# A four-layer graph network on one core: a planner's constants, the first transfers, and the last graph by halves

## The chip, the cores and the metric

The kernel runs on one core of a Trainium2 chip. The metric is the device time of one execution in microseconds, as the median of several runs. The engines are TensorE (PE, with its weight loads as PEld), VectorE (DVE), ScalarE (ACT), GpSimd (POOL) and SyncE (SP), which issues the transfers.

## The reference, cut to what matters

There are 32 independent graphs of 512 nodes with 256 features, each with an adjacency of 512 x 512, all in float32. Every graph goes through four layers, each with a residual and a layer norm:

```python
agg = einsum('bnm,bmd->bnd', adj, x)
# layer 0
x = layernorm(x + relu(((1 + eps) * x + agg) @ W1 + b1) @ W2 + b2)
# layer 1
h = adj @ (x @ W.T + b);  x = layernorm(x + where(h > 0, h, alpha * h))
# layer 2
h = layernorm(x) * g + be
x = layernorm(x + x + relu((adj @ h) @ W_rel + b_rel + h @ W_root))
# layer 3
h = ((epsilon * x + agg) @ W1 + b1)
h = silu(h * rsqrt(mean(h * h) + 1e-6) * w)
x = layernorm(x + h @ W2 + b2)
```

## The kernel before

**Recorded operations and a planner.** The kernel does not issue its instructions as it goes. Every helper (`mm`, `act`, `add`, `mul`, `ts`, `stt`, `copy`, `inv_sqrt`) records an `Op` in a `Plan`, with the engines that could do it and a cost for each; every transfer is recorded by `move`. At the end `Plan.order` goes through time, always takes the engine that is free first, and gives it the recorded operation of the lowest rank among those that can start. `copy` and the scaling of a norm may go to DVE or ACT, all else has one engine. The kernel then issues all operations in the order found, so all of them carry one source line (L295 for operations, L313 for transfers). On the chip each engine keeps that order and waits at semaphores.

**Rank.** An operation's rank is its graph's number times a `period`, plus the time by which `needs` wants it, reckoned back from the matmuls that wait for it. After the graph called `final`, the graphs are spaced by `last` instead of `period`. `RULES` holds pairs of such settings (period, pace, last, near); `best` plans with each and keeps the one whose last operation starts earliest. Up to five graphs (`FLIGHT`) are in work at once, so one graph's matmuls cover another's elementwise work. In `needs` an operation inherits a due time only from consumers of its own graph; graph -1 holds what comes ahead of the first graph, in the kernel before nothing but nine matmuls on zeros.

**Powers and the port.** A norm's inverse square root is a power on POOL (`inv_sqrt`, a tensor_tensor with -0.5). The planner holds back DVE operations with two operands outside PSUM (`TWO_OPERANDS`) for `PORT` microseconds after a DVE operation that feeds a power, so that the power starts undisturbed, and while a power's input is being taken the power holds off in turn. Where DVE has nothing else to do in that time, the planner notes a `pause`, and the kernel issues small memsets to the tile `pause` in its place (L1168).

**Matrix products.** All products go through `seven`, a scheme of seven products of half-size blocks in place of eight. `right_sums` and `left_sums` make the needed sums of blocks on DVE, `take` and `put` bring results out of PSUM. `aggregate` multiplies by the adjacency, `dense_feat` and `dense_add` are the dense layers. `with_loops` adds the self loops (`loop0` = identity times 1 + eps, `loop3`) to the diagonal blocks of the adjacency.

**The start.** SP first issues the adjacency of graph 0 in four transfers of 256 KB, then x in one of 512 KB, then the epsilon of layer 0 (0.5 KB), then weights. DVE makes `one_eps0` and `loop0` from epsilon.

**The end.** In the first and the last graph (`alone()`) layer 3 takes its row norm by `everywhere` with a power and four transposing matmuls on `ident` ("flips"), and its last norm with `NormOnVector` (batch-norm statistics on DVE). `dense_add` calls `norm.half(h)` as each half of the tokens is done, half 1 first; then `norm.scales` makes one power for all four chunks, `norm.scaled` scales them, and one transfer of 512 KB writes the graph.

Of the kernel before, what the change touches and what calls it, by code (L numbers as in the profile page):

```python
# [11 lines left out]
AF = mybir.ActivationFunctionType  # L12
ALU = mybir.AluOpType
# [3 lines left out]
LN_EPS = 1e-5  # L17
# [3 lines left out]
def span(ap):  # L21

    n = 1
    for d in ap.shape[1:]:
        n *= d
    return n
# [13 lines left out]
def vector_time(n):  # L40
    return 0.06 + n * 0.00106, 0.085
# [20 lines left out]
def power_time(n):  # L62
    return 0.3 + n * 0.18, 0.2 + 0.06 * n
# [13 lines left out]


TWO_OPERANDS = ("tensor_add", "tensor_sub", "tensor_mul", "scalar_tensor_tensor")
PORT = 0.35  # L80


SOON = 0.03
# [3 lines left out]

RULES = [(42, 2, 20, 0.5), (42, 2, 12, 0.25)]


class Pool:
# [122 lines left out]
class Plan:  # L218
# [102 lines left out]
    def needs(self, pace, near):  # L321

        work, need = {}, []
        for op in self.ops:
            t = op.ways.get("tensor")
            need.append(work.get(op.graph, 0.0) * pace if t else 1e3)
            if t:
                work[op.graph] = work.get(op.graph, 0.0) + t[0][0]  # L330
        between = [20.0] * len(self.ops)
        for i in range(len(self.ops) - 1, -1, -1):
            op = self.ops[i]
            cost = min(sum(w[0]) for w in op.ways.values()) + 0.1
            for n, _ in op.then:
                if self.ops[n].graph == op.graph:
                    need[i] = min(need[i], need[n] - cost)
                    step = 0.0 if "tensor" in self.ops[n].ways else between[n] + cost
                    between[i] = min(between[i], step)
        return [  # L340
            t if "tensor" in op.ways else t + near * b
            for op, t, b in zip(self.ops, need, between)
        ]

    def best(self):


        rule = min(RULES, key=lambda rule: self.order(*rule)[0])
        return self.order(*rule)[1]

    def order(self, period, pace, last, near):

        final = max(op.graph for op in self.ops) - self.flight + 1
        rank = [
            (min(op.graph, final) * period + max(op.graph - final, 0) * last + need, i)
            for i, (op, need) in enumerate(zip(self.ops, self.needs(pace, near)))
# [14 lines left out]
        done = []  # L371
        while can_start:
# [31 lines left out]
            for i in can_start:  # L404
                op = self.ops[i]
# [17 lines left out]
            op = self.ops[i]  # L423
# [4 lines left out]
            if engine == "vector":  # L428
# [4 lines left out]
                if any(n in powers for n, _ in op.then):  # L433
                    port["vector"] = t + busy + PORT
            if op.kbytes:
# [23 lines left out]
def tile_gnn_stack(ctx: ExitStack, tc: tile.TileContext, a: dict, out: bass.AP):  # L459
# [26 lines left out]
    B, N, D = a["x"].shape  # L486
    NC = N // P
# [5 lines left out]
    HC = NC // 2  # L493
# [8 lines left out]
    plan = Plan(nc, FLIGHT)  # L502
# [24 lines left out]
    def vector(method, n, *args, **kw):  # L527
        return "vector", method, vector_time(n), args, kw

    def scalar(func, n, x, times=scalar_time, **kw):  # L530
        columns = sum(k in ("scale", "bias") and not isinstance(v, float) for k, v in kw.items())
        return "scalar", "activation", times(n, columns), (x,), dict(func=func, **kw)

    def mm(o, lhsT, rhs, first, last):
        kw = dict(start=first, stop=last, skip_group_check=True)
        way = "tensor", "matmul", matmul_time(rhs.shape[-1]), (lhsT, rhs), kw
        plan.do(o, way, ordered=o.room)
# [13 lines left out]
    def add(o, x, y):  # L551
        plan.do(o, vector("tensor_add", span(o), x, y))
# [4 lines left out]
    def mul(o, x, y):  # L557
        plan.do(o, vector("tensor_mul", span(o), x, y))

    def ts(o, x, s1, s2, op0, op1=None):  # L560
        kw = dict(op0=op0) if op1 is None else dict(op0=op0, op1=op1)
        plan.do(o, vector("tensor_scalar", span(o), x, s1, s2, **kw))
# [9 lines left out]
    def inv_sqrt(o, x):  # L572
        n, p = span(o), o.shape[0]
        plan.do(
            o, ("gpsimd", "tensor_tensor", power_time(n), (x, mhalf[0:p, 0:n]), dict(op=ALU.pow))
        )
# [11 lines left out]
    def bank(*shape):  # L588
        return Part(Room(banks)).shaped(*shape)

    def tok():
        return room(NC, D)

    def half(t, h):
        return t[:, h * HC : (h + 1) * HC]
# [16 lines left out]
    def constant(name, shape):  # L612
        return const.tile(shape, F32, tag=name, name=name)
# [15 lines left out]
    def weight(name):  # L629
        w = a[name]  # L630
        t = constant(name, [P, w.shape[0] // P, w.shape[1]])
        size = w.shape[0] * w.shape[1] / 256
        plan.move(t, w.rearrange("(c p) f -> p c f", p=P), size)
        return t
# [5 lines left out]
    scraps = [constant(f"scrap{i}", [P, D]) for i in range(2)]  # L640
# [206 lines left out]
    def dense_add(x, right, left, done):  # L847


        def block(i, j):  # L850
            return x[:, j * HC : (j + 1) * HC, i * P : (i + 1) * P]

        def product(m, ps, first):
            n = len(right[m])
            for k in range(n):
                for i in range(HC):
                    mm(
                        ps[:, i, :], right[m][k][:, i * P : (i + 1) * P], left[m][:, k, :],
                        first and i == 0 and k == 0, k == n - 1,
                    )  # L860

        def take(ps, i, j):
            add(block(i, j), ps, block(i, j))

        def put(ps, i, j, more):
            take(ps, i, j)
            if i == 1:
                done(j)

        seven(*(bank(HC, P) for _ in range(3)), product, take, put)  # L870
# [22 lines left out]
    class Norm:  # L893
# [24 lines left out]
        def scales(self, *affine):  # L918
# [5 lines left out]
            n = len(affine) * NC  # L924
            inv_sqrt(self.rstd[:, 0:n], self.ve[:, 0:n])

        def scaled(self, i=0):

            y = self.r if i == self.last else tok()
            s, shift = (t[:, i * NC : (i + 1) * NC] for t in (self.rstd, self.shift))  # L930
            mul(shift, self.less, s)
            for c in range(NC):
                r, scale = self.r[:, c, :], s[:, c : c + 1]
                plan.do(
                    y[:, c, :],
                    vector(
                        "tensor_scalar", D, r, self.less[:, c : c + 1], scale,
                        op0=ALU.add, op1=ALU.mult,
                    ),
                    scalar(AF.Identity, D, r, scale=scale, bias=shift[:, c : c + 1]),  # L940
                )
            return y

    class NormOnVector(Norm):
# [58 lines left out]
    def plus_row(x, r):  # L1003

        for h in range(2):
            add(half(x, h), half(x, h), r.unsqueeze(1).to_broadcast([P, HC, D]))
# [12 lines left out]

    def load_x(b):  # L1020
        x = tok()
        plan.move(x, a["x"][b].rearrange("(p c) d -> p c d", c=NC), N * D / 256, late=1.6)
        return x

    def layer0(x, adjacency):
# [53 lines left out]
    def layer3(x, adjacency, b):  # L1079

        aT = aggregate(x, adjacency)
        plus_row(x, b2_3)
        hT, acc = Wide(FC3), short(N)

        def squares(f):
            sq = room(2, N)
            act(sq, hT.pair(f), AF.Square)
            if f == 0:
                add(acc, sq[:, 0, :], sq[:, 1, :])
            else:  # L1090
                add(acc, acc, sq[:, 0, :])
                add(acc, acc, sq[:, 1, :])

        dense_feat(aT, A1_3, b1_3, hT, squares)
        pr = everywhere(column_sums(acc), (1.0 / HID3, RMS_EPS, ALU.mult, ALU.add))
        right = {}
        for q in range(0, FH, 2):
            for f in (q, q + 1, FH + q, FH + q + 1):
                mul(hT.chunk(f), hT.chunk(f), pr)
                act(hT.chunk(f), hT.chunk(f), AF.Silu, scale=w_3[:, f : f + 1])  # L1100
            for m, t in dense_sums([hT.pair(q)], [hT.pair(FH + q)]).items():
                right[m] = right.get(m, []) + t
        norm = (NormOnVector if alone() else Norm)(x)
        dense_add(x, right, A2_3, norm.half)
        norm.scales((1.0, LN_EPS))
        y = norm.scaled()
        place = out[b].rearrange("(p c) d -> p c d", c=NC)
        plan.move(place, y, N * D / 256, into=f"out{b}")

# [1 line left out]
    idle, zeros = bank(D), scraps[0]  # L1113
    for _ in range(9):
        mm(idle, zeros[:, 0:P], zeros, True, True)
    plan.graph = 0
    scraps = cycle(scraps)
    eps0 = row("L0_gnn_eps")
    x = load_x(0)
    adjacency = Adjacency(0)  # L1120
    one_eps0 = constant("one_eps0", [P, 1])
    ts(one_eps0, eps0, 1.0, None, ALU.add)
    loop0 = constant("loop0", [P, P])
    ts(loop0, ident, one_eps0, None, ALU.mult)
    W1_0 = weight("L0_gnn_W1")
    A1_0 = weight_sums("A1_0", *quarters(W1_0))
    b1_0 = col("L0_gnn_b1")
# [8 lines left out]
    x = layer0(x, adjacency)  # L1136
# [9 lines left out]
    h = layer1(x, adjacency)  # L1146
# [9 lines left out]
    A2_3 = weight_sums("A2_3", *blocks_of(W2_3[:, 0:FH], W2_3[:, FH:]))  # L1156
    layer3(layer2(*h, adjacency), adjacency, 0)
    for b in range(1, B):
        plan.graph = b
        x, adjacency = load_x(b), Adjacency(b)  # L1160
        h = layer1(layer0(x, adjacency), adjacency)
# [45 lines left out]
```

## Time and profile before

| | us |
|---|---|
| median of 3 runs | 2337.26 |
| lowest and highest | 2336.43, 2342.0 |
| the profiled execution, device time | 2338.08 |
| its span, from first to last instruction | 2336.3 |

The profiled execution is 0.8 us above the median. The page names the busy time of each engine and the costliest groups; since nearly all operations share a line, groups are told apart by the tiles that they write and read: `ps` is a PSUM bank, `room` a large tile of the work pool, `few` a small one for a norm's columns, `scrap` the unused output of an ACT sum. One matmul instruction makes two records in the trace. An idle time in square brackets is the engine's gap ahead of the instruction, with what ended it.

### The profile page before, as it was taken

The page shows a single profiled execution, that of the slowest core. Times are in us where ns is not written, and L with a number is a line of the kernel's source. Part 1 is how long each engine was busy: PE and PEld are TensorE (multiplying, and loading weights), DVE is VectorE, ACT ScalarE, POOL GpSimd, SP SyncE. Part 2 cuts the span into 40 slices and gives each one's busy share as a digit, 9 for nine tenths or more (in the row PEclk, how much of TensorE's full clock was granted, in tenths as well). Part 3 has the DMA queues.
Part 4 walks back from the last instruction along what each step waited for, and adds up shares of the span by engine and source line. Part 5 has one row for each costly group of instructions (what it writes and reads, how often), then busy time and mean ns, then how long its engine had stood idle before and what let it go on. Part 6 is the DMA issues. An engine that isn't in the chain of part 4 may idle for free.

```text
span 2336.3 us, 41057 instructions
## 1 busy us (share of the span) xinstructions
PE 2304.8 (99%) x14002; PEld 2105.4 (90%) x14002; DVE 2139.5 (92%) x5411; ACT 1630.1 (70%) x4409; POOL 261.9 (11%) x166
## 2 busy tenths in 40 slices
PE   9899999999999999999999999999999999999997
PEld 7798999999999999999999999999999999898997
DVE  8998999999999999999999999999999999899987
ACT  4676677766776776777767767767777677676775
POOL 0001101101101101011011011010110101101110
PEclk9999999999999999999999999999999999999999
DMA  7002122122221122211222211222112222121001
GB/s 239 19 19 57 24 57 54 28 56 62 57 60 28 56 57 64 55 47 37 57 62 57 60 27 56 57 63 56 44 38 58 62 60 58 23 65 55 15 17 39
DMA packets 223458, 122.83 MB, mean 53 GB/s; under 512 B 142864, under 2 KB 194320, under 8 KB 223248
## 3 DMA queue, kind: packets, MB, share of 16 engines
q1 hardware_dynamic: 223248, 120.20, 18.8%
q8 instruction: 111, 1.82, 0.3%
q14 instruction: 99, 0.81, 0.1%
HBM read 78.92 MB, written 24.97 MB: 44 GB/s over the span
## 4 chain that ended last, share of the span: by engine, by line
PE 73%; DVE 22%; issue 2%; ACT 2%; DMA 1%; POOL 0%; SPq 0%; DVEq 0%; POOLq 0%; ACTq 0%
PE ps L295 73%; DVE room L295 19%; DVE few L295 2%; ACT room L295 1%; ACT scrap L295 1%; DMA L_gnn_W<-in_L_gnn_W_dram 0%; DMA L_gnn_ln_beta_c<-in_L_gnn_ln_beta_dram 0%; POOL few L295 0%; DMA room<-in_adj_dram 0%; SPq L313 0%; DVE A L295 0%; DVEq L295 0%; POOLq L1203 0%; DVE L_gnn_W_root L295 0%; DVE pause L1168 0%
## 5 line engine op out<-in xcount | busy, mean ns | idle before, releaser
L295 PE MATMUL ps<-room,room 128*128 128x256 f32 x3584 | 920.1, 382 | 6.1 <-DVE room L295 1.9
L295 DVE TENSOR_TENSOR room<-room,room 128x512 f32<-128x512 f32 (+1 forms) x1360 | 783.4, 594 | 7.2 <-ACT room L295 4.4
L295 DVE TENSOR_TENSOR room<-ps,room 128x256 f32<-128x256 f32 (+1 forms) x1344 | 611.1, 470 | 143.3 <-PE ps L295 134.3
L295 PEld LDWEIGHTS ps<-room,room 128*128 128x128 f32 x3584 | 625.6, 191 | 73.7 <-DVE room L295 10.0
L295 PE MATMUL ps<-L_gnn_W,room 128*128 128x128 f32 (+1 forms) x3584 | 539.5, 291 | 6.5 <-ACT room L295 4.5
L295 PEld LDWEIGHTS ps<-L_gnn_W,room 128*128 128x128 f32 x3584 | 505.1, 192 | 39.2 <-ACT room L295 5.7
L295 POOL TENSOR_TENSOR few<-few,mhalf 128x4 f32<-128x4 f32 (+2 forms) x160 | 261.1, 1638 | 2068.7 <-DVE few L295 1969.4
L295 PEld LDWEIGHTS ps<-A,room 128*128 128x128 f32 x3072 | 453.5, 191 | 37.3 <-DVE room L295 3.7
L295 PE MATMUL ps<-A,room 128*128 128x128 f32 x3072 | 467.3, 275 | 1.6 <-DVE room L295 1.5
L295 PE MATMUL ps<-room,L_gnn_W 128*128 128x256 f32 x1536 | 419.8, 381 | 0.6 <-DVE room L295 0.5
L295 ACT ACTIVATE room<-room,few 128x256 f32<-128x256 f32 x590 | 316.7, 595 | 114.2 <-DVE few L295 113.1
L295 ACT ACTIVATE room<-room 128x1024 f32<-128x1024 f32 (+2 forms) x260 | 241.5, 941 | 165.2 <-DVE room L295 159.5
L295 ACT ACTIVATE room<-ps,L_gnn_b_c 128x256 f32<-128x256 f32 x768 | 309.9, 476 | 49.2 <-PE ps L295 42.2
L295 ACT ACTIVATE room<-ps 128x256 f32<-128x256 f32 (+1 forms) x515 | 180.6, 377 | 232.5 <-PE ps L295 231.5
L295 PE MATMUL ps<-room,A 128*128 128x256 f32 x1152 | 332.6, 381 | 5.5 <-ACT room L295 5.4
L295 DVE TENSOR_TENSOR room<-room 128x256 f32<-128x256 f32 (+1 forms) x640 | 312.9, 498 | 10.6 <-ACT room L295 3.0
L295 PEld LDWEIGHTS ps<-room,L_gnn_W 128*128 128x128 f32 x1536 | 276.3, 191 | 34.9 <-DVE room L295 2.5
L295 ACT ACTIVATE scrap<-room 128x256 f32<-128x256 f32 x504 | 206.7, 411 | 93.9 <-DVE room L295 84.2
L295 ACT ACTIVATE scrap<-room,few 128x256 f32<-128x256 f32 x504 | 251.9, 502 | 27.4 <-DVE few L295 25.4
L295 PEld LDWEIGHTS ps<-room,A 128*128 128x128 f32 x1152 | 198.9, 191 | 23.3 <-ACT room L295 6.7
L295 ACT ACTIVATE room<-room,L_gnn_rms_weight_c 128x512 f32<-128x512 f32 x256 | 173.6, 714 | 14.5 <-DVE room L295 14.3
L295 DVE TENSOR_TENSOR room<-room,loop 128x256 f32<-128x256 f32 x256 | 103.4, 411 | 4.1 <-PE ps L295 2.3
(57 smaller groups left out, 1131.7 us busy)
## 6 DMA issues: line engine op xcount, KB each, us to landing
room<-in_adj_dram SPq DMA_DIRECT2D x128, 256.0 KB, 5.1
room<-in_x_dram SPq DMA_DIRECT2D x32, 512.0 KB, 5.9
out_dram<-room SPq DMA_DIRECT2D x32, 512.0 KB, 3.1
room<-room SPq DMA_DIRECT2D x480, 32.0 KB, 2.0
diagonal<-room SPq DMA_DIRECT2D x62, 128.0 KB, 1.8
room<-in_adj_dram SPq DMA_DIRECT2D x124, 64.0 KB, 1.9
room<-diagonal SPq DMA_DIRECT2D x62, 128.0 KB, 2.2
room<-line SPq DMA_DIRECT2D x30, 256.0 KB, 3.2
```

The lines of the kernel that those rows point to most:

```text
L295: getattr(getattr(self.nc, engine), method)(to, *(put(x) for x in args), **kw)
```

## The change

Five edits in one:

1. `PORT` goes from 0.35 to 0.55.
2. The two `RULES` have `last` 10 and 16 in place of 20 and 12, both with `near` 0.5, and `final` is the highest graph less `LATE` = 3, so that graphs 29, 30 and 31 are spaced by `last` (before, four graphs).
3. The epsilon transfer, `one_eps0` and `loop0` are recorded in graph -1, and `needs` lets graph -1 inherit due times from any graph.
4. The first graph's x comes in two transfers of 256 KB.
5. The last graph finishes by halves: `finish` makes the scale, the power, the scaled chunks (`put`) and the transfer of each half as soon as its sums are there.

```diff
-PORT = 0.35
+PORT = 0.55
...
-RULES = [(42, 2, 20, 0.5), (42, 2, 12, 0.25)]
+LATE = 3
+RULES = [(42, 2, 10, 0.5), (42, 2, 16, 0.5)]
...
-                if self.ops[n].graph == op.graph:
+                if op.graph in (self.ops[n].graph, -1):
...
-        final = max(op.graph for op in self.ops) - self.flight + 1
+        final = max(op.graph for op in self.ops) - LATE
...
+        def finish(self, h, m, plus, place):
+
+            mine = slice(h * HC, (h + 1) * HC)
+            ve, rstd, shift = self.ve[:, mine], self.rstd[:, mine], self.shift[:, mine]
+            ts(ve, self.squares[:, mine], m / self.n, plus, ALU.mult, ALU.add)
+            inv_sqrt(rstd, ve)
+            mul(shift, self.less[:, mine], rstd)
+            for c in range(h * HC, (h + 1) * HC):
+                self.put(c, self.r, rstd[:, c % HC : c % HC + 1], shift[:, c % HC : c % HC + 1])
+            plan.move(place, half(self.r, h), N * D / 512, into=f"out{plan.graph}{h}")
...
-        plan.move(x, a["x"][b].rearrange("(p c) d -> p c d", c=NC), N * D / 256, late=1.6)
+        src = a["x"][b].rearrange("(p c) d -> p c d", c=NC)
+        if b:
+            plan.move(x, src, N * D / 256, late=1.6)
+        else:
+            for h in range(2):
+                plan.move(half(x, h), half(src, h), N * D / 512, late=1.6)
...
-        dense_add(x, right, A2_3, norm.half)
-        norm.scales((1.0, LN_EPS))
-        y = norm.scaled()
         place = out[b].rearrange("(p c) d -> p c d", c=NC)
-        plan.move(place, y, N * D / 256, into=f"out{b}")
+        if b < B - 1:
+            dense_add(x, right, A2_3, norm.half)
+            norm.scales((1.0, LN_EPS))
+            y = norm.scaled()
+            plan.move(place, y, N * D / 256, into=f"out{b}")
+        else:
+
+            def done(h):
+                norm.half(h)
+                norm.finish(h, 1.0, LN_EPS, half(place, h))
+
+            dense_add(x, right, A2_3, done)
...
-    plan.graph = 0
-    scraps = cycle(scraps)
     eps0 = row("L0_gnn_eps")
-    x = load_x(0)
-    adjacency = Adjacency(0)
     one_eps0 = constant("one_eps0", [P, 1])
     ts(one_eps0, eps0, 1.0, None, ALU.add)
     loop0 = constant("loop0", [P, P])
     ts(loop0, ident, one_eps0, None, ALU.mult)
+    plan.graph = 0
+    scraps = cycle(scraps)
+    x = load_x(0)
+    adjacency = Adjacency(0)
```

More of the change, by code (lines that the diff above doesn't have):

```diff
@@ L925, in scales, with put @@
             inv_sqrt(self.rstd[:, 0:n], self.ve[:, 0:n])
+        def finish(self, h, m, plus, place):
[7 more added lines that the diff above has]
+            plan.move(place, half(self.r, h), N * D / 512, into=f"out{plan.graph}{h}")
+        def put(self, c, y, scale, shift):
+            r = self.r[:, c, :]
+            plan.do(
+                y[:, c, :],
+                vector(
+                    "tensor_scalar", D, r, self.less[:, c : c + 1], scale, op0=ALU.add, op1=ALU.mult
+                ),
+                scalar(AF.Identity, D, r, scale=scale, bias=shift),
+            )
         def scaled(self, i=0):
@@ L932, in scaled @@
             for c in range(NC):
[L933 to L941, printed above, removed]
+                self.put(c, y, s[:, c : c + 1], shift[:, c : c + 1])
             return y
```

## The prediction

> **What bounds the kernel now.** I read the page first, then two steady windows, then the timeline where TensorE (PE) was idle.
>
> ```profile
> PE 2304.8 (99%) x14002; PEld 2105.4 (90%) x14002; DVE 2139.5 (92%) x5411; ACT 1630.1 (70%) x4409; POOL 261.9 (11%) x166
> ```
>
> ```profile
> 1210.91:1282.38 71.47, 71.39 (x436) 65.49 (x436) 66.01 (x167) 51.08 (x140) 8.46 (x6) 1.00 0.19 53
> 1282.38:1353.85 71.47, 71.39 (x436) 65.49 (x436) 66.03 (x167) 51.09 (x140) 8.46 (x6) 1.00 0.20 53
> ```
>
> The first line is the page's busy times. The columns of the two windows are length, then busy time of PE, its weight loads, DVE, ACT and POOL, then clock. One graph takes 71.47 us and PE is busy for 71.39 of it. In the trace a PE record of 256 columns follows the last after 216 ns, one of 128 columns after 112 ns; the program has 6810 and 7192 of them, so 1471 + 806 = 2277 us of pure streaming. The span is 2336.3, so **about 59 us are stalls**. One steady graph has 212 and 224 records, 45.8 + 25.1 = 70.9 us, so it loses only 0.6, some 15 us over 25 graphs. The rest lies at the two ends. What can be won is there; what can be lost is mostly in the middle, because anything lost per graph is multiplied.
>
> The losses at the start, from the timeline (start, length, engine, operation, idle before it and its releaser):
>
> ```profile
> 9.22 0.15 DVE L295 TENSOR_SCALAR one_eps<-L_gnn_eps 128x1 f32<-128x1 f32 x1 [3.60 <-DMA L_gnn_eps<-in_L_gnn_eps_dram]
> ...
> 11.38 3.72 PE L295 MATMUL ps<-room,room 128*128 128x256 f32 x16 [1.64 <-DVE room L295]
> ```
>
> DVE stands still for 3.60 us because a half-kilobyte vector lies behind 1.5 MB in the queue, and PE gets its second operand only at 11.38. Later, around 100 us:
>
> ```profile
> 100.93 0.46 ACT L295 ACTIVATE room<-ps,L_gnn_b_c 128x256 f32<-128x256 f32 x1
> ...
> 104.62 0.46 ACT L295 ACTIVATE room<-ps,L_gnn_b_c 128x256 f32<-128x256 f32 x1
> ...
> 105.13 2.08 PE L295 MATMUL ps<-room,A 128*128 128x256 f32 x4 [5.11 <-ACT room L295]
> ```
>
> and a window behind it, clock third from the end:
>
> ```profile
> 104.90:108.30 3.40, 3.17 (x8) 2.54 (x9) 3.01 (x11) 3.40 (x11) 1.36 (x1) 0.50 0.00 0
> ```
>
> PE waits 5.11 us for the second of two evictions of a bank by ACT; six norm sums stand between the two on ACT. Then the clock is granted at 0.50 for 3.4 us (the window), which costs another 1.7. At the end:
>
> ```profile
> 2306.29 2.05 PE L295 MATMUL ps<-L_gnn_W,room 128*128 128x128 f32 x16 [0.52 <-DVE room L295]
> ...
> 2310.13 0.65 PE L295 MATMUL ps<-ident,few 128*128 128x128 f32 x4 [1.79 <-POOL few L295]
> ...
> 2313.01 7.25 PE L295 MATMUL ps<-L_gnn_W,room 128*128 128x128 f32 x48 [2.23 <-ACT room L295]
> ...
> 2326.14 2.05 PE L295 MATMUL ps<-L_gnn_W,room 128*128 128x128 f32 x16 [0.52 <-DVE room L295]
> ...
> 2331.38 1.09 ACT L295 ACTIVATE room<-room,few 128x256 f32<-128x256 f32 x2 [5.38 <-DVE few L295]
> 2332.50 0.33 SPq L313 DMA_DIRECT2D out_dram<-room  x1
> ```
>
> In the last graph PE waits for the row norm's power, for the SiLUs behind it, and for DVE. After the four flips of `everywhere` only that graph's 56 output products are left, so nothing fills the waits.
>
> **What the Trainium skill says.** "TensorE: Matmul & The Clock Gate" (What's actually happening) says that an idle window of some 3.4 us halves the clock until PE has been busy for about as long. The trace agrees: 0.50 in 104.9 to 108.3 after the 5.11 us wait. "SBUF — State Buffer" (Who interferes with whom) says that a DVE instruction with two SBUF inputs contends with a GpSimd one that reads SBUF. The trace agrees, rarely: a power of four columns takes 1.01 us as a rule, but 2.32 at 283.54 and 2.04 at 2035.94, both beside DVE adds of two SBUF tiles. This is what PORT plans around.
>
> **The change part by part.** The order of both programs on every engine shows what the planner makes of it.
>
> *Epsilon first, x in halves.* The epsilon transfer is now SP's first issue, `one_eps0` and `loop0` are DVE's first work. Epsilon goes ahead of the adjacency by one issue, 0.43 us, and x is one issue more, 0.43. Before, the second half of the adjacency was there by about 7.3 (ACT's third copy starts at 7.28); now about 7.7. Then four DVE operations lead to PE's second product: two of 512 columns and two of 256, 0.60 and 0.34 from start to start, 1.9 us: 9.6 instead of 11.38. I take **-1.7**. Bounds: 0, since the DMA engines are 84 to 87% busy through the first 50 us and later loads may set the pace, and -2.2. DVE is 98% busy from 25 to 100 us, which is why I believe that an earlier DVE survives.
>
> *The order around 100 us.* PE's instructions up to the wait are the same products in the same order. On ACT the first of the two evictions moves ahead of its norm sums, and the second moves ahead of six sums that stood before it. In the old times the second would start when the sums now left ahead of it are over, at about 101.3 instead of 104.62. **-3.4** (bounds 0, if PE then waits for DVE, which was 92% busy there, and -5.1, if the half clock goes too).
>
> *The last three graphs at 10, from graph 29 on.* The planner chose period 20 before and chooses 10 now. Behind the flips 93 products of 128 columns now follow instead of 56: 37 of other graphs, 37 x 0.223 = 8.3 us of filler, 10 of them (2.2 us) before the first one that needs a SiLU. Ahead of the flips stand some 50 products of the other two graphs. So the waits of 0.68, 1.95 and 2.39 us (by start to start) and the 1.7 of half clock at 2313 go, 6.7 in sum; about 1.0 comes back, since two multiplications of 0.60 and two SiLUs of 0.65 on a queue take 3 us against 2.2 of filler. The last 0.68 stays. **-5.7**. Bounds -6.7 and -2: 24 norm sums (0.46 from start to start), 14 scalings (0.5) and 8 SiLUs (0.65) of three graphs now stand on ACT at once, about 23 us beside 21 of PE.
>
> *Norm and output by halves.* From the last product to the end were 8.1 us. The last power has two columns instead of four (1.01 us for four, 1.64 for eight, so about 0.7, -0.3) and ACT scales one chunk instead of two behind it (-0.5). But the neighbouring graph's three chunks now stand ahead of it on ACT (+0.9), its 512 KB ahead of the last 256 KB (+0.3), and two small DVE operations are added (+0.15). **+0.5**, bounds -1 and +1. Out by halves alone would save; its cover is gone because the other graphs end in the same 5 us.
>
> *PORT 0.55.* It is a number in the planner. 22 memsets of `pause` become 72: one per graph through the middle, 33 in DVE's last 600 of 4979 rows. Each takes 0.10 to 0.18 us of DVE. In the middle DVE has 5.5 us free per graph and is relieved of one operation that goes to ACT: 0. In the last stretch 33 x 0.15 = 5 us of DVE, where graphs bunch: before, the bunching at 2032 to 2040 already cost PE 1.1 + 1.5 and a half-clock window. I take **+1.5**, bounds -3 (some powers are no longer held up) and +8.
>
> *The middle.* The planner's order no longer repeats with every graph but with every second one; PE's order agrees with the old one for about 88%. DVE is level with PE in 14 us of each graph (the chain runs over DVE from 1268 to 1282, over PE for 55). Taken as **0**; it cannot gain over 0.6 x 25 = 15.
>
> Sum: -1.7 - 3.4 - 5.7 + 0.5 + 1.5 = -8.8 on the profiled execution's 2338.1, so 2329.3. The median of the runs is 0.8 below that execution: 2328.5, say **2329**.
>
> **Rivals.**
> 1. *Only the ends give.* The wait at 100 us returns under another name (bank, DVE) and the bunching eats half of the tail: -1.7 - 3.5 + 1 = -4, 2333. For it: DVE and ACT are both over 90% busy at 100 us. Against: ACT's order there is plainly better.
> 2. *The middle loses: slower.* The alternating order with a pause per graph adds waits to the 14 us where DVE and PE are level. It decides the sign where it exceeds 0.35 us per graph (8.8 / 25), and passes 0.3% from 0.63 us per graph, a doubling of today's loss. At 0.75 it gives 2328.5 + 19 = 2347. For it: the multiplier. Against: one DVE operation less, and evictions now go first behind the powers' producers.
> 3. *More than I count.* The half clock at 105 goes too and the middle sheds a third of its stalls: -8.8 - 1.7 - 5, 2322.
> 4. *The edits do little*: the first loads are bound by DMA, the tail by ACT: 2337. The order shows that the edits are made, so this is the far end of rival 1.
>
> **How the numbers follow.** 0.3% of 2337 is 7.0 us, about what a measurement of this kernel can tell from no change: faster means below 2330.2, slower above 2344.3. Forecast 0.50 (2323 to 2334; four fifths of it faster); rivals 1 and 4 together 0.28 (2331 to 2340, nearly all the same); rival 3 0.10; rival 2 0.12. Faster 0.40 + 0.03 + 0.10 = 0.53, same 0.10 + 0.25 = 0.35, slower 0.12. The range 2321 to 2341 leaves out most of rival 2 and the edge of rival 3.
>
> **What would show it.** One_eps before 4 us, PE's second product before 10; no PE wait over 2.5 us at 100; a steady pair of graphs in 143 us; no wait over 1.5 us among PE's last 200 records, and ACT near full there; the last output 8 to 9 us after PE's last product. I am wrong if a pair takes over 144, or if PE waits over 6 us in sum where the last three graphs bunch.

## The result, and the profile after

| | before | after |
|---|---|---|
| median of 4 runs each, us | 2339.61 | 2319.62 |
| lowest and highest | 2336.43, 2342.0 | 2318.51, 2320.4 |
| the profiled execution | 2338.08 | 2319.3 |
| its span | 2336.3 | 2317.5 |

The ratio is 0.9915 (95% interval 0.9903 to 0.9928): **faster, by 0.85%**. The direction was the forecast's. The size was not: 2319.6 lies 9.4 us below the 2329 and 1.4 us below the range.

The page's busy times after:

```profile
PE 2295.5 (99%) x14002; PEld 2089.9 (90%) x14002; DVE 2120.0 (91%) x5428; ACT 1642.6 (71%) x4444; POOL 256.9 (11%) x167
```

This line hardly moves, and it can't show the gain: PE is "99% busy" in both. The two steady windows do (length, then busy time of PE, PEld, DVE, ACT and POOL, then clock):

```profile
1203.41:1274.60 71.19, 71.19 (x439) 65.06 (x437) 65.39 (x167) 51.44 (x141) 8.27 (x6) 1.00 0.20 53
1274.60:1345.78 71.18, 71.18 (x439) 65.06 (x437) 65.39 (x167) 51.45 (x141) 8.26 (x6) 1.00 0.20 53
```

A graph takes 71.18 us instead of 71.47. That is 0.28 us, over 25 graphs 7 us, and the prediction had put it at nothing. (In such a line the numbers behind the clock are the busy share of the DMA engines and GB/s.)

To place the rest I add up TensorE's stalls: for each pair of consecutive PE records, the time from start to start less the 216 or 112 ns of its width, where that exceeds 60 ns (a half clock counts in it). Each column is one profiled execution.

| stretch, us | before | after | change | the prediction's step |
|---|---|---|---|---|
| 0 to 110 | 17.0 | 12.1 | -5.0 | start -1.7, order at 100 us -3.4 |
| 110 to 300 | 3.3 | 5.2 | +1.9 | - |
| 300 to 1900 | 16.0 | 7.1 | **-8.9** | the middle 0 |
| 1900 to 2290 | 7.7 | 6.2 | -1.6 | PORT in the last stretch +1.5 |
| from 2290 | 7.6 | 0.8 | -6.8 | last three graphs -5.7 |
| after PE's last product | 8.4 | 8.8 | +0.4 | halves +0.5 |

The changes sum to -19.8 (-20.0 from the rounded rows), and the span fell by 18.8. The 1.0 between them lies in differences of under 60 ns a record, which this sum leaves out.

Two rows hold more chance than the others. From 1900 to 2290, 1.4 of the 1.6 is a half clock that the profiled execution of before has from 2036.8 to 2040.2, behind waits of 1.14 and 1.47 us. Four runs below that change nothing there (product 267 first, eviction 273 first, both, and the quicker powers) have the same two waits, the full clock behind them and stalls of 6.3 to 6.4. The first 20 us differ by 2 us from execution to execution, as the section on the prediction's steps shows. The middle does not: over the runs below, three profiles with the old order there have 15.3 to 16.0, and four with the new one 7.1 to 7.2.

The start, from the timeline of after:

```profile
3.33 0.15 DVE L298 TENSOR_SCALAR one_eps<-L_gnn_eps 128x1 f32<-128x1 f32 x1 [1.36 <-DMA L_gnn_eps<-in_L_gnn_eps_dram]
...
9.16 4.55 PE L298 MATMUL ps<-room,room 128*128 128x256 f32 x20 [2.33 <-DMA room<-in_x_dram]
...
18.25 1.10 PE L298 MATMUL ps<-L_gnn_W_rel,L_gnn_ln_beta_c 128*128 128x256 f32 x4 [1.08 <-DMA L_gnn_ln_beta_c<-in_L_gnn_ln_beta_dram]
```

One_eps is there at 3.33 instead of 9.22, and PE runs through from 9.16 where it had stood from 9.7 until 11.38. But at 18.25 it waits 1.08 us for a transfer of 1 KB. Around 100 us:

```profile
99.39 0.70 PE L298 MATMUL ps<-room,room 128*128 128x256 f32 x2 [1.45 <-DVE room L298]
...
102.72 1.13 PE L298 MATMUL ps<-room,room 128*128 128x256 f32 x4 [0.26 <-DVE room L298]
```

and the window that had shown clock 0.50:

```profile
104.90:108.30 3.40, 3.40 (x23) 2.69 (x21) 3.32 (x13) 3.40 (x10) 1.64 (x1) 1.00 0.00 0
```

The wait of 5.11 us for ACT is gone, the half clock with it, and what is left there is two waits for DVE. At the end:

```profile
2306.90 2.05 PE L298 MATMUL ps<-L_gnn_W,room 128*128 128x128 f32 x16 [0.52 <-DVE room L298]
```

That is the only gap of PE after 2290. The waits for the power and for the SiLUs are filled by the neighbouring graphs.

### The profile page after: what moved, and what is told of

The parts are those of the page before. It is cut to its first block, busy times and chain, and to the rows that moved or that the text cites. A ratio compares the mean times of both kernels' runs of the same rounds, so it can differ in the third digit from the quotient of the medians.

```text
span 2317.5 us, 41158 instructions
## 1 busy us (share of the span) xinstructions
PE 2295.5 (99%) x14002; PEld 2089.9 (90%) x14002; DVE 2120.0 (91%) x5428; ACT 1642.6 (71%) x4444; POOL 256.9 (11%) x167
## 3 DMA queue, kind: packets, MB, share of 16 engines
q1 hardware_dynamic: 223536, 120.20, 19.1%
## 4 chain that ended last, share of the span: by engine, by line
PE 89%; DVE 7%; ACT 2%; DMA 1%; issue 1%; SPq 0%; POOL 0%; ACTq 0%; DVEq 0%
PE ps L298 89%; DVE room L298 6%; ACT room L298 1%; ACT scrap L298 1%; DVE few L298 1%; DMA room<-in_x_dram 1%; DMA L_gnn_W<-in_L_gnn_W_dram 0%; DMA room<-in_adj_dram 0%; DMA L_gnn_b<-in_L_gnn_b_dram 0%; DMA diagonal<-room 0%; SPq L316 0%; ACT L298 0%; DVE A L298 0%; DVE L_gnn_W_root L298 0%; POOL few L298 0%
## 5 line engine op out<-in xcount | busy, mean ns | idle before, releaser
L298 PE MATMUL ps<-room,room 128*128 128x256 f32 x3584 | 930.9, 381 | 5.7 <-DVE room L298 3.2
L298 DVE TENSOR_TENSOR room<-room,room 128x512 f32<-128x512 f32 (+1 forms) x1360 | 773.0, 590 | 5.4 <-ACT room L298 2.8
L298 PEld LDWEIGHTS ps<-room,room 128*128 128x128 f32 x3584 | 617.3, 191 | 70.3 <-DVE room L298 7.1
L298 PEld LDWEIGHTS ps<-A,room 128*128 128x128 f32 x3072 | 460.5, 191 | 47.3 <-DVE room L298 14.1
L298 PE MATMUL ps<-A,room 128*128 128x128 f32 x3072 | 486.9, 276 | 0.9 <-DVE room L298 0.7
L298 POOL TENSOR_TENSOR few<-few,mhalf 128x4 f32<-128x4 f32 (+2 forms) x161 | 256.2, 1598 | 2054.5 <-DVE few L298 1883.1
L298 ACT ACTIVATE room<-room,few 128x256 f32<-128x256 f32 x627 | 335.0, 596 | 159.9 <-DVE few L298 159.7
L298 PE MATMUL ps<-room,A 128*128 128x256 f32 x1152 | 320.0, 380 | 1.1 <-ACT room L298 0.8
```

Source lines behind the costliest of these rows:

```text
L298: getattr(getattr(self.nc, engine), method)(to, *(put(x) for x in args), **kw)
```

## The experiments

Ratios are to runs of before on the same chip in the same group. The median of before lay between 2337.3 and 2339.6 over the groups, so a distance to the changed kernel, which ran in another group, says little under 2 us.

### The parts, one by one

**PORT alone** in the kernel before:

```diff
-PORT = 0.35
+PORT = 0.55
```

> The kernel before with PORT 0.55 alone. Its plan has the changed kernel's two alternating orders in the middle, the old order around 100 us (second eviction behind six sums) and the old spacing of 20 at the end. Theory A (PORT makes the middle, the start edits make the ends' first part, the spacing makes the tail): a pair of steady graphs takes 142.4 us instead of 142.9, so about 8 us less in the middle, nothing at either end: 2329 to 2332 against 2338. Rival B (the middle sheds because of how the whole program starts or ends, PORT itself does nothing or costs a memset per graph): a pair stays at 142.9 or more, 2337 to 2342.

Measured: 2329.4 us, 0.9962 (0.9948 to 0.9977) of before, whose median in this group of runs was 2337.9. So a planner's constant that the prediction priced at +1.5 gives **-8.5**. Stalls from 300 to 1900 are 7.1, as in the changed kernel; those from 2290 stay at 7.7. The same 714 us of the middle, first of before, then of this run (PE's records are in the first brackets):

```profile
1200.00:1914.00 714.00, 713.16 (x4352) 653.56 (x4351) 659.00 (x1658) 509.69 (x1389) 84.63 (x50) 1.00 0.20 53
```

```profile
1200.00:1914.00 714.00, 714.00 (x4376) 652.35 (x4375) 656.10 (x1664) 513.58 (x1396) 82.72 (x50) 1.00 0.20 53
```

PE gets through 24 records more in the same time.

**PORT undone** in the changed kernel (`PORT = 0.35`):

> The changed kernel with PORT back at 0.35. Its plan has the old single order in the middle, the new order around 100 us and the new spacing at the end. Theory A: 142.9 us for a pair of steady graphs, about 8 us lost in the middle, the wait at 100 us stays short and the tail stays full: 2327 to 2330. Rival B: the middle keeps 142.4 and the time stays at 2319 to 2322.

Measured: 2333.3, 0.9979 (0.9971 to 0.9987), that is 13.7 above the changed kernel. Stalls from 300 to 1900 are back at 15.6, and so is the number of PE's records:

```profile
1200.00:1914.00 714.00, 712.99 (x4352) 653.85 (x4351) 659.27 (x1660) 509.33 (x1388) 83.66 (x50) 1.00 0.20 53
```

The other parts, together, are worth only 4.6 without it. The next run gives 4.8 for the rules alone, so with PORT at 0.35 the start's edits and the halves together gain nothing: ahead of 110 us the stalls are 16.2 instead of 19.7 with the rules alone, but from 110 to 300 us 7.4 instead of 4.3.

**The rules alone** in the kernel before:

```diff
-RULES = [(42, 2, 20, 0.5), (42, 2, 12, 0.25)]
+LATE = 3
+RULES = [(42, 2, 10, 0.5), (42, 2, 16, 0.5)]
...
-        final = max(op.graph for op in self.ops) - self.flight + 1
+        final = max(op.graph for op in self.ops) - LATE
```

> The kernel before with the new RULES and LATE = 3 alone: the last three graphs at 10, everything until graph 28 in the old order. Theory A: the waits ahead of and behind the flips go (6.8 us) and the bunching near 2030 is redrawn: 2329 to 2333, all of the difference after 1900 us. Rival B (the tail was only won because PORT holds powers clear of DVE where three graphs bunch): 2334 to 2338, with powers of over 2 us and PE waits of over 1.5 us in the last 300 us.

Measured: 2333.05, 0.998 (0.9972 to 0.9989), -4.8. From 2290 stalls fall from 7.6 to 1.9, while the time behind PE's last product grows from 8.4 to 9.7; the middle keeps its 15.3. All gaps of PE from 2280 on, from the timeline of this run:

```profile
2304.51 1.32 PE L296 MATMUL ps<-L_gnn_W,room 128*128 128x128 f32 x8 [0.72 <-ACT room L296]
2321.54 2.05 PE L296 MATMUL ps<-L_gnn_W,room 128*128 128x128 f32 x16 [0.52 <-DVE room L296]
```

One wait for the SiLUs comes back, as predicted; with PORT at 0.55 it goes too.

**The start undone** in the changed kernel (epsilon, `one_eps0` and `loop0` back behind x, x whole, `needs` as before):

> The changed kernel with the start undone: adjacency, x in one transfer, then epsilon, and graph -1 without due times. Its plan has the second eviction behind six sums again. Theory A: the wait of about 5 us and the half clock behind it are back at 100 us, so 2319.6 + 5 = 2324 to 2326, the middle and the tail unchanged. Rival B (the wait at 100 us is set by PORT): PE waits no more than 2 us there and the time is within 2 us of the changed kernel's.

Measured: 2323.85, 0.9937 (0.9922 to 0.9952), 4.2 above the changed kernel. The wait at 100 us is back, with a half clock behind it. PE in the timeline, and a window behind its wait:

```profile
106.64 2.07 PE L298 MATMUL ps<-room,A 128*128 128x256 f32 x4 [5.46 <-ACT room L298]
```

```profile
104.70:108.00 3.30, 1.36 (x3) 1.17 (x4) 2.30 (x8) 3.24 (x14) 1.01 (x1) 0.50 0.01 2
```

So the start's edits are what reorders ACT at 100 us. The changed kernel pays 2.3 of it back between 110 and 300 us, where its stalls are 5.2 against 2.9 here.

**The finish undone** (the last graph's norm and output whole again, as before):

> The changed kernel with the last graph's norm and output whole again, as before. The prediction put the halves at +0.5 us (bounds -1 to +1): this would give 2319.1, between 2318.6 and 2320.6. A rival, that the halves hide the first half's norm and transfer under the last products and that only DVE's queue hid the gain: 2321 or more without them.

Measured: 2320.36 (2319.43 to 2321.59) against the changed kernel's 2318.51 to 2320.4: not told apart. From PE's last product to the end are 9.05 us instead of 8.84, so the halves are worth 0.2 us here. The traces leave no room for the rival's larger gain.

**No memsets**: the changed kernel in the same order, with the pauses not issued.

```diff
-            if op.pause and op.way == "vector":
-                for _ in range(round(op.pause / 0.11)):
-                    nc.vector.memset(pause, 0.0)
```

> The changed kernel with its order on every engine and none of the 72 memsets to the tile pause. Theory A (PORT works through the order that it makes: evictions from PSUM stand behind a power's producer, and the memsets are small change): within 2 us of 2319.6, a pair of steady graphs at 142.4. Rival C (it works because the memsets really hold DVE off): powers behind the missing memsets go from 1.01 to over 1.5 us and the time rises to 2323 or more.

Measured: **2317.75** (2317.0 to 2318.63), 0.9909 (0.9894 to 0.9924), the lowest of all and 1.9 below the changed kernel, so it beats before surely and the changed kernel by about what two groups can differ. The traces tell them apart: stalls from 1900 to 2290 are 4.7 here and 5.0 in the last run below, which has no memsets either, against 6.0 to 6.4 in the six profiles of the changed kernel's order there with them. The memsets cost what the prediction said and buy nothing: the eight-column powers take 1.64 us without them as with them. PORT helps by the order that it leads the planner to, not by the pauses.

### Why PORT changes the middle: what it is not

**VectorE relieved.** PORT 0.55 also gives one operation per graph (526, a norm's scaling) to ACT. `YIELD`, the planner's preference for ACT, does that in the kernel before (`YIELD = 2.0` for 0.8):

> The kernel before with YIELD 2.0 in place of 0.8, PORT still 0.35: the one scaling of a graph that DVE took goes to ACT, as with PORT 0.55. Theory D (the middle gains because DVE has one operation of 0.4 us less in each graph): a pair of steady graphs near 142.4 and 2329 to 2332. Theory A (the gain is in the order around the powers): the power of eight columns still takes 2.58 us, a pair stays within 0.2 of 142.9, and the time within 3 us of 2338.

Measured: 2348.55, 1.0042 (1.0027 to 1.0056), slower. The steady graph's waits are the same (0.245, 0.105, 0.085, 0.13, 0.075 us), so the relief isn't it. The 10 us that it loses lie outside the middle: stalls are 10.0 from 110 to 300 us and 9.8 from 1900 to 2290, against 3.3 and 7.7. Why the relief may be worth nothing, the windows further down show: 526 stands last ahead of VectorE's idle time.

**Shorter powers.** In 24 graphs of the kernel before, two memsets ahead of VectorE's operation 138, so that the eight-column power behind it starts undisturbed:

```diff
+        eights = {587 + 528 * (g - 1) + 138 for g in range(4, 28)}
+        held = {id(plan.ops[i]) for i in eights}
         for op in plan.best():
+            if id(op) in held:
+                for _ in range(2):
+                    nc.vector.memset(pause, 0.0)
```

> The kernel before, its order untouched, with two memsets on DVE ahead of the addition that starts 0.07 us after each steady graph's power of eight columns (graphs 4 to 27). Theory C (contention for the port is what costs time): the power goes from 2.58 to about 1.64 us, and the middle gains in spite of 0.35 us more on DVE: a pair at 142.6 or less, 2332 to 2335. Theory A (order): the power gets shorter too, but no PE wait depends on it, and DVE's 0.35 us is either hidden or lost: a pair at 142.9 to 143.6, 2338 to 2346.

Measured: 2341.8, 1.0017 (1.001 to 1.0024), slower. GpSimd in the timeline, first of before, then of this run:

```profile
1241.52 3.55 POOL L295 TENSOR_TENSOR few<-few,mhalf 128x8 f32<-128x8 f32 x2 [10.52 <-DVE few L295]
```

```profile
1244.02 1.64 POOL L295 TENSOR_TENSOR few<-few,mhalf 128x8 f32<-128x8 f32 x1 [10.51 <-DVE few L295]
1246.04 1.01 POOL L295 TENSOR_TENSOR few<-few,mhalf 128x4 f32<-128x4 f32 x1 [0.39 <-DVE few L295]
```

The two powers took 3.55 us back to back and take 1.64 + 1.01 now: they are quicker, and the kernel isn't. No wait of TensorE got shorter by more than 0.01 us, and the one at product 52 (below) grew from 0.14 to 0.30 us a graph, since VectorE's eviction ahead of it comes 0.17 us later behind the memsets. That powers slow down beside VectorE agrees with the Trainium skill, "SBUF — State Buffer" (Who interferes with whom). It was not rare, as the prediction had it from the four-column powers: the eight-column ones of before take 2.28 us on average. But in this order no wait of TensorE hung on it. In the changed kernel the eight-column powers are down to 1.64 us as here, and the four-column ones up from 1.04 to 1.20.

**Any redraw.** The changed kernel with `PORT = 0`:

> The changed kernel with PORT 0: no operation is held for a power, no memset is planned. If holding matters at all (theory A and C), powers of eight columns take about 2.6 us and a pair of steady graphs 142.9 or more, 2326 to 2336. If the middle improved merely because the plan was redrawn and 0.35 happened to be a bad draw (theory E), PORT 0 is as good as 0.55: a pair at 142.4, 2318 to 2323.

Measured: 2346.42, 1.0028 (1.0017 to 1.0039), slower, by the first 300 us: stalls are 19.1 from 110 to 300. From 300 to 1900 they are 13.8, below before's 16.0 and far from 7.1. So it takes a good draw, not a new one.

### What the middle's order does: single places moved

VectorE is the engine to look at. Windows of one steady graph of before, cut where VectorE first stands still:

```profile
1195.33:1255.35 60.02, 59.94 (x377) 55.20 (x376) 59.37 (x155) 45.17 (x129) 8.47 (x5) 1.00 0.11 31
1255.35:1266.29 10.94, 10.94 (x60) 9.85 (x59) 6.20 (x10) 5.39 (x11) 0.00 (x0) 1.00 0.67 180
```

and the same of after:

```profile
1187.60:1247.11 59.51, 59.51 (x376) 54.56 (x375) 58.92 (x156) 45.26 (x129) 8.27 (x5) 1.00 0.10 26
1247.11:1258.51 11.40, 11.40 (x62) 10.26 (x61) 6.19 (x11) 5.90 (x13) 0.00 (x0) 1.00 0.70 202
```

The third busy time is VectorE's. Its "92% busy" is **99% through 60 us of each graph and 57% in the remaining 11**. In the 60 us both engines are full, and TensorE waits wherever an eviction stands behind other work on VectorE. Before, there are five waits per graph: 0.25 and 0.10 us at the two records of the aggregate product 239, for eviction 238; 0.09 at product 143, whose operands come from ACT and by transfer; and 0.14 + 0.08 at product 52, for eviction 27. PE in before at the first, and 3 us on:

```profile
1281.47 0.83 PE L295 MATMUL ps<-L_gnn_W_root,room 128*128 128x128 f32 x6
1282.38 1.13 PE L295 MATMUL ps<-room,room 128*128 128x256 f32 x4
...
1285.79 1.97 PE L295 MATMUL ps<-A,room 128*128 128x128 f32 x16
```

Six records of 112 ns end their turn 0.67 after 1281.47, at 1282.14; the next starts at 1282.38. After has two W_root records more in that place (product 267), which fill the wait. It is left with three waits of 0.10, one at 239 and two at product 289.

**Product 267 first**, in 22 graphs of the kernel before (the numbers are those of a graph's 528 recorded operations; 267 makes two records, not the four that the expectation says):

```diff
+        ops, chosen = plan.ops, plan.best()
+        for g in range(4, 26):
+            first = 587 + 528 * (g - 1)
+            chosen.remove(ops[first + 267])
+            chosen.insert(chosen.index(ops[first + 239]), ops[first + 267])
-        for op in plan.best():
+        for op in chosen:
```

> The kernel before, with one TensorE product moved in 22 graphs (4 to 25): the fourth W_root product (operation 267 of its graph, four 128-column records) is issued ahead of the aggregate product (239) that waits for a DVE eviction, as the order of the changed kernel has it, not two products after it. DVE, ACT, GpSimd and SP keep their orders. Theory A (the gain of the middle is the place of this product, which fills the wait at operation 239): the wait of 0.25 us a graph falls to about 0.1 or below, 22 x 0.15 to 0.22 = 3.3 to 4.8 us, so 2333 to 2335 us against 2338. Theory B (the order on DVE decides, the product's place is incidental): the wait reappears somewhere else in the same graph and the time stays at 2337 to 2339.

Measured: 2337.93, 1.0003 (0.9994 to 1.0011), no change. Theory A fails here. PE at the same places:

```profile
1283.32 1.05 PE L295 MATMUL ps<-L_gnn_W_root,room 128*128 128x128 f32 x8
1284.24 1.13 PE L295 MATMUL ps<-room,room 128*128 128x256 f32 x4
...
1287.42 2.19 PE L295 MATMUL ps<-A,room 128*128 128x128 f32 x16
```

Eight records, 0.90, and the next starts at 0.92: that wait is filled. But the sixteen A records now take 2.19 instead of 1.97 us; a wait of 0.17 + 0.07 is inside them, at product 284, for eviction 273 on VectorE.

**The same product put back** in the changed kernel (267 behind 240):

> The changed kernel, with the same product (267) put back behind the aggregate products (239, 240) in graphs 4 to 25 and nothing else changed. Theory A: the wait comes back, 3 to 5 us, so 2323 to 2325 us against 2319.6. Theory B: no change, 2319 to 2320.5.

Measured: 2327.02, 0.9949 (0.9932 to 0.9965), 7.4 above the changed kernel: more than theory A's 3 to 5. The wait of 0.25 returns and two smaller ones with it, about 0.41 us a graph. So the place is needed, and alone it is worth nothing.

**Eviction 273 first as well**: product 267 first and, on VectorE, the 128x512 multiplication 262 behind 273.

```diff
+            chosen.remove(ops[first + 262])
+            chosen.insert(chosen.index(ops[first + 273]) + 1, ops[first + 262])
```

> The kernel before with two instructions moved in graphs 4 to 25, as the changed kernel orders them: TensorE's product 267 ahead of 239 (as in the run with that alone), and VectorE's 128x512 multiplication 262 (0.60 us) from ahead of the eviction 273 to right behind it. In the run with the product alone, the wait of 0.25 us was filled but came back 4 us later as 0.169 + 0.073 us at the A product 284, which waits for the eviction 273. Theory A2 (two places together, one on each engine, make the gain: a wait filled on TensorE is lost again at the next eviction of VectorE that stands behind other work): both waits gone, 22 x 0.245 = 5.4 us, 2331 to 2333 us against 2337.5. Theory B2 (VectorE is full in this stretch and the wait moves on once more): within 1 us of before.

Measured: 2337.48, 0.9996 (0.9987 to 1.0005), no change. Both waits are gone, and two of 0.10 stand 2 us later in their place. B2, not A2.

**That alone**, in the kernel before:

> The kernel before with only the VectorE move (262 right behind 273) in graphs 4 to 25. Theory A2: TensorE still waits 0.25 us at 239, and no wait at 284 was there to be taken: 2337 to 2338.5 us, no change. A rival (the order on VectorE alone makes the gain): 2332 to 2334.

Measured: 2338.0, 0.9997 (0.9989 to 1.0006), no change, as A2 and B2 both have it.

**Undone** in the changed kernel (262 ahead of 273):

> The changed kernel with only VectorE's 262 put back ahead of the eviction 273 in graphs 4 to 25. Theory A2: the wait comes back at the A product 284, 22 x 0.15 to 0.3 = 3 to 6.5 us, so 2323 to 2326 us against 2319.6. Theory B2: within 1 us of 2319.6.

Measured: 2320.28 (2319.46 to 2320.76), B2 again. A wait of 0.19 + 0.07 comes at 284, but two of 0.10 behind it go, so a graph loses 0.06.

**Eviction 27 early**: the last wait of before's stretch, attacked in the kernel before with TensorE's products 25 and 26 ahead of 344 and VectorE's eviction 27 ahead of 165.

```diff
+            move(first + 1081, first + 344, 0)
+            move(first + 1082, first + 344, 0)
+            move(first + 1083, first + 1221, 0)
```

(`move(i, to, behind)` takes an operation out and puts it ahead of or behind another; 528 stands for each graph ahead.)

> The kernel before. In its trace VectorE has no gap over 0.11 us from 1194.8 to 1255.4 us of every graph's 71.5 us, and its idle time lies in the 11 us after that. TensorE's last wait within that full stretch is at operation 52 of the graph two ahead (0.137 + 0.075 us at 1245.57), for VectorE's eviction 27. Moved here, in 22 graphs: the two TensorE products 25 and 26 ahead of 344 of the older graph, and with them eviction 27 ahead of operation 165, that is about 1.5 us of VectorE's work earlier, as the changed kernel has it. Theory F (the last wait of the full stretch sets the sum; waits ahead of it only shift): that wait goes, 22 x 0.21 = 4.7 us, 2333 us against 2338. A rival (the wait reappears elsewhere once more): within 1 us of before.

Measured: 2343.74, 1.0018 (1.0011 to 1.0024), **slower** by 4.4, where theory F wanted 4.7 faster. The wait at 52 is gone. The next comes 2 us on, twice as long, and for another engine. PEld and ACT in the timeline of this run:

```profile
1252.03 0.30 PEld L295 LDWEIGHTS ps<-room,A 128*128 128x128 f32 x2 [0.33 <-ACT room L295]
```

```profile
1249.18 2.08 ACT L295 ACTIVATE room<-room,few 128x256 f32<-128x256 f32 x4
1251.16 0.82 ACT L295 ACTIVATE room<-ps,L_gnn_b_c 128x256 f32<-128x256 f32 x2
```

TensorE now comes to these products before ACT has emptied their bank, and ACT's evictions stand behind four scalings.

**All three places** in the kernel before:

> The kernel before with that move and the two of the earlier run (product 267 ahead of 239, multiplication 262 behind eviction 273). Theory F: with the last wait gone, the two earlier moves, worth nothing without it, now pay: 0.25 us more a graph, 22 x (0.21 + 0.2) = 9 us, so 2328 to 2330 us. The rival: within 1 us of before, or of the run with the move of 27 alone.

Measured: 2343.39, 1.0019 (1.0012 to 1.0026), as with eviction 27 alone. Theory F is out.

**Eviction 27 put back** in the changed kernel:

> The changed kernel with products 25 and 26 put back behind 38 and eviction 27 put back ahead of operation 242 in 22 graphs. Theory F: TensorE, which is ahead of VectorE here, waits again at operation 52: at least 22 x 0.1, up to 22 x 0.3 us, so 2322 to 2326 us. The rival: within 1 us of 2320.

Measured: 2326.19, 0.9943 (0.9928 to 0.9957), 6.6 above the changed kernel, at the upper end of what F gave. But the wait of 0.15 + 0.10 us a graph came at an earlier product (344), not at 52, so F's mechanism isn't confirmed by it.

**Three loop additions deferred**, an attempt at a better version (from the kernel without memsets):

```diff
+            move(first + 311, first + 1102, 1)
+            move(first + 313, first + 1102, 1)
+            move(first + 314, first + 1102, 1)
```

> The changed kernel without the memsets, and with three 0.34 us loop additions of VectorE (operations 311, 313, 314, first read some 25 us later) put behind the multiplication 46 of the graph two ahead, so that 1.0 us of work no longer stands ahead of the evictions that TensorE waits for at 0.10 + 0.10 us a graph. Theory F, if the end of VectorE's full stretch has slack in this order: 22 x 0.2 = 4.4 us, 2313 to 2314 us against 2317.8. If the end has none, the wait moves there: 2317 to 2318.

Measured: 2335.68, 18 above the kernel that it started from. VectorE, ACT and PE in its timeline:

```profile
1222.86 1.08 DVE L298 TENSOR_TENSOR room<-room,loop 128x256 f32<-128x256 f32 x3
...
1224.57 1.33 ACT L298 ACTIVATE room<-room,L_gnn_rms_weight_c 128x512 f32<-128x512 f32 x2 [1.10 <-DVE room L298]
...
1225.34 0.92 PE L298 MATMUL ps<-L_gnn_W,room 128*128 128x128 f32 x4 [0.32 <-ACT room L298]
```

The 1.0 us of additions stands where ACT waits for VectorE and TensorE for ACT, and costs 0.49 us at that one product, of 0.77 us a graph in all. The two waits of 0.10 that it was to remove are still there; so this work ahead of the evictions didn't make those.

**What is shown, and what stays open.** Shown: the middle's gain comes with PORT alone, by the order. It is not from the pauses or the relief of one operation, and shorter powers alone gave none. TensorE and VectorE are full for 60 us of each graph, so a filled wait reappears at the next operation that stands behind something else; two of the changed order's places, put back singly, cost 7.4 and 6.6 us, a third nothing. Not shown: which smallest set of places makes the gain, since up to three of them put into the kernel before gave nothing or a loss. One sign was at hand and not used: the planner's own time for its last operation, which `best` minimizes, comes out below that of before for every planned order here that measured faster, and above it for the two that measured slower (YIELD at 2.0 and PORT at 0). It is a reckoning from the kernels and no measurement, and it doesn't give the sizes.

## Why the prediction was right and wrong, by its steps

- **Start and order at 100 us, -1.7 - 3.4: right in size, but in part by luck.** Undone, they cost 4.2. Up to 20 us the stalls of the two profiled executions differ by 0.45 only, but these stalls scatter: from 5.9 to 8.1 (median 7.0) over the eleven profiles with the old start, from 5.1 to 7.3 (median 5.6) over the nine with the new one, so about -1.4. The wait at 18.25 for a transfer of 1 KB takes part of it back, as the reason for the bound of 0 had it. At 100 us the half clock goes too, which only the bound and rival 3 had. What the step left out is the price behind it, some 2 us from 110 to 300 us; with PORT at 0.35 it eats the whole gain, and the prediction names nothing here that depends on PORT.
- **The last three graphs at 10, -5.7: right.** The rules alone take 5.7 off the stalls from 2290 on and 4.8 off the time, since they add 1.3 behind the last product (the prediction had 1.2 of this, the neighbour's chunks and transfer, under the halves); with PORT it is 6.8. The last wait stays at 0.68 by start to start, as said.
- **Halves, +0.5: right**, +0.4 from PE's last product to the end. Without the halves it is 9.05: they save 0.2, and the cover that went costs 0.65.
- **PORT in the last stretch, +1.5: the price was right, the sum wrong.** The memsets cost 1.4 there. The order around them saves 3.0 against before's profiled execution, but 1.4 of that is its half clock; against the four profiles of the same two waits at the full clock it saves 1.6 and just pays for the memsets.
- **The middle, 0, and with it PORT's 0 for the middle: this step failed**, by 8.9 of stalls, where PORT alone gave -8.5 us. The bound of 15 held; the value came from a misread view. "DVE is level with PE in 14 us" was taken from the chain of waits, which follows PE wherever PE's own wait is short. The windows show VectorE at 99% for 60 of 71.5 us. In such a stretch the order decides 0.3 to 1.1 us per graph either way (0.30 in after, 0.65 in before, 1.1 with the additions deferred), so 0 had no support, and a redraw of the order should have been given both signs.
- **Rivals.** Rival 3 named what happened, the half clock and the middle, at 2322: its third of the middle's stalls was over half (16.0 to 7.1). It got a chance of 0.10. Rival 2 would have shown in a steady pair of over 144 us; it is 142.37.

## What to carry to other kernels

Cut an engine's busy share at its idle gaps before calling it free: 92% was 99% for most of a period. Where two engines are both full, price a new order as a draw with both signs and the size of all present waits, and don't expect a better one from filling the wait that is seen, as it moves to the next eviction in line. And when a planner's constant helps, test whether the thing it plans for matters: here the pauses cost about 1.4 us and were not needed.

## What the runs showed of the hardware

A GpSimd power on eight columns takes 2.58 us in the steady graphs of before, where VectorE's next addition of two SBUF tiles starts 0.07 us after it, and 1.64 in the run with memsets ahead of that addition, where it starts 0.30 us after; in both, two such additions run beside the power. So the loss hangs on the power's first moments and not on the overlap as such. It is GpSimd's alone: the additions took 0.42 us beside the slowed power, as others of their size did with no power running. I had expected some of it on VectorE's side too.

That TensorE's clock halves behind an idle stretch of some 3.4 us is the Trainium skill's "TensorE: Matmul & The Clock Gate" (What's actually happening). The runs agree where the wait is long: 0.50 behind waits of 5.1 and 5.5 us. But two shorter waits close together had it too, and not always: in before the clock is 0.50 behind 1.95 and 2.39 us at 2313, and behind 1.14 and 1.47 us at 2036.8, where four runs with the same two waits kept 1.00. The changed kernel, whose longest wait after 20 us is 1.6, had no half clock while it had products to do.
